# A two-layer graph network on Trainium2: the leaky step of layer 1 on ScalarE and GpSimd, the halves of q and k on GpSimd, three pieces of work in other slots

## The chip, the cores and the metric

The kernel runs on one core of one Trainium2 chip. The metric is the time of one execution in microseconds (us), the median of several runs; lower is better. A core has five engines, each with its own queue of instructions that it works through in order: TensorE (PE in the profile, its weight loads apart as PEld), VectorE (DVE), ScalarE (ACT), GpSimd (POOL) and SyncE (SP, which here only issues DMAs). An instruction waits, with everything behind it on its engine, until the semaphores that it names have been raised.

## The reference

The input is x (16 graphs, 1024 nodes, 256 features, fp32) and an adjacency matrix of zeros and ones (16 x 1024 x 1024, int32). Two layers run, each on a normed input with a residual:

```python
h = jnp.maximum(_layernorm(x), 0.0)           # layer 0: attention with 8 heads of 32
Q, K, V = proj(Wq, bq), proj(Wk, bk), proj(Wv, bv)
scores = where(adj == 0, -inf, einsum('bhnd,bhmd->bhnm', Q, K) * SCALE)
x = x + einsum('bno,po->bnp', softmax(scores) @ V, Wo) + bo
h = jnp.maximum(_layernorm(x), 0.0)           # layer 1: scores from a_0, leaky relu, slope 0.2
e = leaky_relu(einsum('bid,bjd->bij', h * a_0[:, 0], h), 0.2)
x = x + softmax(where(adj == 1, e, -9e15)) @ h
```

Kinds of edges above 1 (a_1 to a_3) would need further scores; a general path behind a test at the end (`layer_1_of_kinds`) covers them and does not run for these inputs.

## The kernel before

Layer 0's unit of work is an attention tile: 128 rows (queries) of one graph, all 8 heads, 1024 columns (`Attend`). There are 16 x 8 = 128 of them, and the main loop takes one *step* for each (`for s in range(B * NT + 1)`; t is the tile's number in its graph, 0 to 7). Within a step `for h in range(HEADS)` goes through the heads. For each head TensorE makes the scores of 128 x 1024 in one of two PSUM tiles called sides (`scores`, L455: two matmuls of 512 columns), DVE reads that side, scales, masks and finds the row maximum (`softmax_max`, L467), ScalarE exponentiates (`softmax_exp`, L475), and the result is transposed: for heads 2, 3, 6, 7 by TensorE with two copies of ScalarE (`turn`, L574 and L575), for heads 0, 1, 4, 5 by a DVE block transpose (`turn_blocks`, L376) and four DMAs of SyncE (`place_blocks`, L381). `combine` (L510) multiplies by the values, for heads 0 to 3 at h = 7 and for heads 4 to 7 at h = 3 of the next step. Then follow `output` (L525), `residual` (L531) and the norm's statistics on DVE.

Three more kinds of work share the step. *Pieces* (`Piece`) prepare 128 rows of a later graph: load, norm, transpose, then projections of k, q and v. The projections of k and q are written as two fp32r parts, a rounded high part by ScalarE (`high`, L289) and the rest by DVE (`split`, L294). They go to DRAM (k twice, once by SyncE at L321 and once by GpSimd in `write_again`; q by `write_queries`, L315) and come back in another layout (`load_key`, L356; `load_queries`, L422). *Layer 1's norm*: `norm_of`, 18 small GpSimd instructions on the statistics of one layer 0 tile and one piece together; then `normed` on ScalarE (L542), `turn_normed` on TensorE (L549), `turned_normed` on ScalarE (L553). *Edge tiles* (`Edges`) are layer 1's 128 rows, nine steps behind layer 0; in a step with tile t, the edge tile is number t - 1 of its graph (7 for t = 0). Its scores fill one side in two halves (`score`, L610 and L616: blocks left of the diagonal are transposed from copies kept in `mirror`, the rest are matmuls); `keep` (L630, ScalarE) copies blocks to `mirror`; `softmax_max` (L639, DVE) writes the negated scores y = -e, masked with a very large number, to `sel` and the smallest y of a row to `top`; `leak` (L647, DVE) makes min(0.2 y, y), that is, the negated leaky relu. Then come the exponential (L651), the block transpose and placements, `gather` (L669) and `store` (L678).

The order is written by hand (`tc.manual_schedule()`): each engine's queue holds its instructions in the order of the Python calls, nothing is moved later. Two sides for nine score tiles a step mean that the edge tile holds side 1 from after head 7 of the step before until its DVE pass and mirror copies are done, and heads 0, 1, 2 share side 0 meanwhile. Buffers set further waits: `blocks` has three, `sel`, `adj` and `xb` one each.

At t = 7 and t = 0, the *batch boundary*, GpSimd also issues the eight key loads of the next graph (512 KB each), at places set by `KEY_STEPS` (2h for the start and 2h + 1 for the end of head h; 16 and more lie in the t = 0 step). Before the loop lies a prologue; in the first nine steps there are no edge tiles; after the loop eight edge tiles are left, which run alone.

## Time and profile before

| | |
|---|---|
| time, median of 3 runs | 3197.36 us (3194.01 to 3206.88) |
| the profiled execution's own time | 3201.33 us |
| its span in the profile | 3199.5 us |
| PE busy | 2955.3 us (92%) |
| DVE busy | 2797.0 us (87%) |
| ACT busy | 2509.5 us (78%) |
| POOL busy | 1755.1 us (55%) |
| granted TensorE clock, mean | 0.987 |
| first and last residual addition (L531, one a step) | 101.0 and 3120.6 us |

The span is the time from the first instruction to the last in the profiled execution. Between the first and the last residual addition lie 127 steps, so a step takes 23.8 us on average. Cut at each step's first score matmul, the steps of batches 2 to 13 take, for t = 0 to 7: 24.87, 24.37, 24.33, 23.86, 23.34, 23.12, 23.34 and 25.44 us on average. A row of grouped instructions gives the line, the engine, the operation, the tiles written and read, the shape and the count, then the busy time and the mean of one in ns, then the idle time of the engine just before them and what ended it. In a timeline the first number is the start in us from the span's beginning, the second the duration. Ends of matmuls are modelled, so PE's busy time can cover a short wait.

### The profile page before, as it was taken

The page shows a single profiled execution, that of the slowest core. Times are in us where ns is not written, and L with a number is a line of the kernel's source. Part 1 is how long each engine was busy: PE and PEld are TensorE (multiplying, and loading weights), DVE is VectorE, ACT ScalarE, POOL GpSimd, SP SyncE. Part 2 cuts the span into 40 slices and gives each one's busy share as a digit, 9 for nine tenths or more (in the row PEclk, how much of TensorE's full clock was granted, in tenths as well). Part 3 has the DMA queues.
Part 4 walks back from the last instruction along what each step waited for, and adds up shares of the span by engine and source line. Part 5 has one row for each costly group of instructions (what it writes and reads, how often), then busy time and mean ns, then how long its engine had stood idle before and what let it go on. Part 6 is the DMA issues. An engine that isn't in the chain of part 4 may idle for free. (4 is left out here: it accounts for less than half of the span.)

```text
span 3199.5 us, 98068 instructions
## 1 busy us (share of the span) xinstructions
PE 2955.3 (92%) x36210; PEld 2215.4 (69%) x36210; DVE 2797.0 (87%) x5111; ACT 2509.5 (78%) x5037; POOL 1755.1 (55%) x3883
## 2 busy tenths in 40 slices
PE   5878999999999999989999999999999999998897
PEld 3666767777776777767767677777777767676664
DVE  3888989989898998989989899898989889898884
ACT  2888878888787888878888788888888788787772
POOL 2555555655555565555655555565565555555442
PEclk8999999999999999999999999999999999999999
DMA  6787787888878788787878888788787878878663
GB/s 225 223 248 228 233 263 225 265 237 233 268 234 274 223 250 254 228 262 234 264 236 237 273 229 279 223 246 261 230 279 227 252 235 240 266 226 269 175 189 94
DMA packets 747157, 762.93 MB, mean 238 GB/s; under 512 B 71280, under 2 KB 692208, under 8 KB 746672
## 3 DMA queue, kind: packets, MB, share of 16 engines
q1 hardware_dynamic: 678432, 542.34, 58.1%
q0 software_dynamic: 65040, 210.03, 20.7%
q8 instruction: 291, 4.77, 0.6%
q10 hardware_dynamic: 3200, 4.19, 0.4%
q14 instruction: 194, 1.59, 0.1%
HBM read 252.98 MB, written 167.77 MB: 132 GB/s over the span
## 5 line engine op out<-in xcount | busy, mean ns | idle before, releaser
L475 ACT ACTIVATE p<-p,nmx 128x1024 f32<-128x1024 f32 x1024 | 1183.4, 1156 | 246.5 <-DVE nmx L467 244.8
L467 DVE CUSTOM_DVE_ANT_0 p<-s,neg 128x1024 f32<-128x1024 f32 x1024 | 1232.9, 1204 | 94.7 <-issue 58.6
L455 PE MATMUL s<-k,qt 128*128 128x512 f32 x2048 | 786.1, 465 | 134.5 <-DMA qt<-qd 59.9
L435 POOL TENSOR_SCALAR neg<-adj 128x1024 bf16<-128x1024 int32 x128 | 467.1, 3649 | 378.7 <-ACT neg L447 378.5
L376 DVE STREAM_TRANSPOSE blocks<-p 128x1024 f32<-128x1024 f32 x520 | 642.9, 1236 | 12.2 <-ACT p L651 10.6
L575 ACT COPY pT<-trp 128x512 f32<-128x512 f32 x1024 | 546.5, 586 | 106.6 <-PE trp L574 103.9
L510 PE MATMUL acc<-pT,v 128*32 128x128 f32 x16384 | 527.2, 275 | 29.1 <-DMA pT<-blocks 27.9
L574 PE MATMUL trp<-ident,p 128*128 128x128 f32 x4096 | 536.0, 274 | 0.3 <-ACT pT L575 0.3
L574 PEld LDWEIGHTS trp<-ident,p 128*128 128x128 f32 x4096 | 483.1, 141 | 71.5 <-issue 1.8
L455 PEld LDWEIGHTS s<-k,qt 128*128 128x128 f32 x2048 | 327.6, 191 | 293.7 <-issue 96.5
L510 PEld LDWEIGHTS acc<-pT,v 128*32 128x32 f32 x16384 | 449.6, 110 | 103.5 <-issue 42.9
L669 PE MATMUL acc<-h,pT 128*32 128x256 f32 x8192 | 504.3, 383 | 15.4 <-DMA pT<-blocks 7.9
L669 PEld LDWEIGHTS acc<-h,pT 128*32 128x32 f32 x8192 | 244.4, 110 | 225.4 <-issue 59.4
L494 POOL COPY wide<-rec 128x256 f32<-128x256 f32 x128 | 51.1, 399 | 478.2 <-DVE rec L492 471.0
L321 POOL DMA_DIRECT2D kd<-halves x240 | 169.1, 704 | 257.6 <-DVE halves L294 244.6
L616 PE MATMUL s<-h1T,ha 128*128 128x512 f32 (+2 forms) x744 | 277.5, 496 | 8.6 <-ACT mirror L630 8.0
L639 DVE CUSTOM_DVE_ANT_0 sel<-s,neg 128x1024 f32<-128x1024 f32 x120 | 146.5, 1221 | 87.8 <-ACT p L475 59.7
L475 ACT ACTIVATION_READ_ACCUMULATOR p<-p,nmx 128x1 f32 x1024 | 199.1, 194 | 0.0
L616 PEld LDWEIGHTS s<-h1T,ha 128*128 128x128 f32 x744 | 122.9, 191 | 73.9 <-issue 46.2
L273 PEld LDWEIGHTS acc<-hT,wkT 128*128 128x128 f32 x960 | 118.4, 194 | 76.7 <-issue 46.5
L273 PE MATMUL acc<-hT,wkT 128*128 128x128 f32 x960 | 141.6, 291 | 27.4 <-DVE halves L294 26.2
L630 ACT COPY mirror<-s 128x128 f32<-128x128 f32 (+3 forms) x208 | 76.3, 395 | 103.0 <-DVE top L639 90.8
(129 smaller groups left out, 4237.7 us busy)
## 6 DMA issues: line engine op xcount, KB each, us to landing
pT<-blocks SPq DMA_DIRECT2D x2560, 128.0 KB, 3.1
qt<-qd SPq DMA_DIRECT2D x128, 512.0 KB, 5.9
adj<-in_adj POOLq DMA_DIRECT2D x127, 512.0 KB, 5.4
qd<-halves SPq DMA_DIRECT2D x240, 256.0 KB, 4.3
k<-kd POOLq DMA_DIRECT2D x120, 512.0 KB, 6.8
kd<-halves POOLq DMA_DIRECT2D x240, 128.0 KB, 3.5
kd<-halves SPq DMA_DIRECT2D x240, 128.0 KB, 3.2
xb<-in_x POOLq DMA_DIRECT2D x128, 128.0 KB, 3.4
```

The source lines that it names most:

```text
L273: nc.tensor.matmul(ps, lhsT=wT[:, fc, oc * P : (oc + 1) * P], rhs=(self.hT, self.hTm)[which][:, fc, :], start=(fc == 0), stop=(fc == NC - 1),)
L321: queue.dma_start(out=kds[self.b][oc, :, :, twice, self.cols], in_=halves.rearrange("p (w n) -> p w n", w=2),)
L376: nc.vector.transpose(blocks.rearrange("p b j q -> p j b q"), p)
L435: nc.gpsimd.tensor_scalar(self.neg, self.adj, 0.0, MASKED, ALU.is_equal, ALU.mult)
L455: nc.tensor.matmul(self.ps[:, cols], lhsT=self.qt[:, h, :], rhs=keysets[self.b][h][:, cols], start=True, stop=True,)
L467: nc.vector.tensor_tensor_reduce(out=p, in0=sides[h in (3, 5, 7)], in1=self.neg, scale=-SCALE, scalar=FLOOR, op0=ALU.add, op1=ALU.min, acc ...
L475: nc.scalar.activation(p, p, AF.Exp, bias=nmx, scale=-1.0, accum_out=self.sums[:, h : h + 1])
L510: nc.tensor.matmul(sums_place[r * HD : (r + 1) * HD, g * P : (g + 1) * P], lhsT=vs[self.b][:, j, place_of(h) : place_of(h) + HD], rhs=self ...
L574: nc.tensor.transpose(tr[:, j, :], p[:, jj * P : (jj + 1) * P], ident)
L575: copy(pT[:, half * 4 : half * 4 + 4, :], tr)
L616: nc.tensor.matmul(self.side[:, cols], lhsT=self.ha[:, c, :], rhs=h1T[:, c, cols], start=(c == 0), stop=(c == NC - 1),)
L669: nc.tensor.matmul(sums_place[a * HD : (a + 1) * HD, :], lhsT=self.pT[:, j, a], rhs=h1s[self.b][:, j, :], start=(j == 0), stop=(j == NT - 1),)
```

## The change

The change has five parts.

1. *The leaky step* of all edge tiles but the last eight. `softmax_max` now scales by -0.2, so `sel` holds z = 0.2 y (still the masked ones a very large number). The result wanted is min(z, 5 z) = z - relu(-4 z). `bend` makes relu(-4 z) with one ScalarE activation into a new tile `less` (a turn of the `blocks` buffers); `leak` subtracts it on GpSimd, after two tiny GpSimd instructions that do the same for the row's smallest value. The two DVE instructions (L644, L647) go. The last eight keep DVE's form.
2. *The halves of q and k.* In the loop, `high` and `split` give way to `raised` (ScalarE writes the biased projection, both chunks, to `full`) and `halve` (GpSimd copies `full` to the fp32r high part and subtracts). k's two chunks are now written by SyncE and GpSimd together at h = 0. Buffers of `halves`: 2 of double size instead of 4.
3. *Layer 1's scores*: the second half at h = 2 instead of 1, the DVE pass at h = 3 instead of 2, the mirror copies at h = 1 and 3 instead of 1 and 2; side 1 now goes to heads 4 and 6 (before: 3, 5, 7).
4. *q's projection* at h = 1 instead of 3, its ScalarE and GpSimd parts at h = 4.
5. *The norm of layer 1*: ScalarE's `normed` at h = 0 of the next step instead of h = 7, the transposes at h = 1 instead of 0 and in another PSUM quarter, the copy at h = 2 instead of 1.

```diff
--- before.py
+++ after.py
@@ -207,7 +207,7 @@
             tag = self.tags[i]
             if tag == "pT":
                 return ptp.tile(shape, dtype, tag=tag, name=tag)
-            bufs = {"p": 4, "blocks": 3, "halves": 4, "qt": 2, "xin": 2}.get(tag, 1)
+            bufs = {"p": 4, "blocks": 3, "halves": 2 if self.n == 1 else 4, "qt": 2, "xin": 2}.get(tag, 1)
             return work.tile(shape, dtype, tag=tag, name=tag, bufs=bufs)
         def load(self, queue=nc.gpsimd):
@@ -310,6 +310,25 @@
             else:
                 self.queries.append((oc, halves))
+        def raised(self, which):
+            self.full = work.tile([P, NC, P], F32, tag="full", name="full", bufs=1)
+            for _ in range(NC):
+                _, oc, ps, bias = self.projected.pop(0)
+                nc.scalar.activation(self.full[:, oc], ps, AF.Identity, bias=bias[:, oc : oc + 1])
+        def halve(self, which):
+            halves = self.buffer(3, [P, NC, 2, P], F32R)
+            nc.gpsimd.tensor_copy(halves[:, :, 0], self.full)
+            nc.gpsimd.tensor_tensor(halves[:, :, 1], self.full, halves[:, :, 0].bitcast(F32), ALU.subtract)
+            places = [(oc, halves[:, oc].bitcast(F32).rearrange("p w n -> p (w n)")) for oc in range(NC)]
+            if which == 0:
+                for oc, place in places:
+                    self.write_keys(oc, place, nc.sync, 0)
+                self.again = places
+            else:
+                self.queries = places
         def write_queries(self):
             for oc, halves in self.queries:
                 nc.sync.dma_start(
@@ -449,7 +468,7 @@
             )
         def scores(self, h):
-            self.ps = sides[h in (3, 5, 7)]
+            self.ps = sides[h in (4, 6)]
             for nh in range(N // HALF):
                 cols = slice(nh * HALF, (nh + 1) * HALF)
                 nc.tensor.matmul(
@@ -465,7 +484,7 @@
             p = work.tile([P, N], F32, tag="p", bufs=4)
             nmx = small.tile([P, 1], F32, tag="nmx")
             nc.vector.tensor_tensor_reduce(
-                out=p, in0=sides[h in (3, 5, 7)], in1=self.neg, scale=-SCALE, scalar=FLOOR,
+                out=p, in0=sides[h in (4, 6)], in1=self.neg, scale=-SCALE, scalar=FLOOR,
                 op0=ALU.add, op1=ALU.min, accum_out=nmx,
             )
             self.probs[h] = (p, nmx)
@@ -544,7 +563,7 @@
             )
         def turn_normed(self):
-            tr = by_chunk(early)
+            tr = by_chunk(brief)
             for c in range(NC):
                 nc.tensor.transpose(tr[:, c, :], h1s[self.b][:, self.t, c * P : (c + 1) * P], ident)
             self.h1_ps = tr
@@ -579,7 +598,7 @@
         def __init__(self, b, t, last=False):
-            self.b, self.t = b, t
+            self.b, self.t, self.last = b, t, last
             self.rows = slice(t * P, (t + 1) * P)
             self.side = sides[t % 2 if last else 1]
             self.tags = {"sel": ("p", 4), "pT1": ("pT", 7)} if last else {}
@@ -635,16 +654,28 @@
         def softmax_max(self):
             self.sel = self.buffer("sel", [P, N])
-            top = small.tile([P, 1], F32, tag="top")
+            self.top = small.tile([P, 1], F32, tag="top")
             nc.vector.tensor_tensor_reduce(
-                out=self.sel, in0=self.side, in1=masks[self.b, self.t], scale=-1.0, scalar=3e38,
-                op0=ALU.add, op1=ALU.min, accum_out=top,
-            )
+                out=self.sel, in0=self.side, in1=masks[self.b, self.t], scale=-SLOPE, scalar=3e38,
+                op0=ALU.add, op1=ALU.min, accum_out=self.top,
+            )
+        def bend(self):
+            if not self.last:
+                self.less = work.tile([P, N], F32, tag="blocks", name="less", bufs=3)
+                nc.scalar.activation(self.less, self.sel, AF.Relu, scale=1 - 1 / SLOPE)
+        def leak(self):
             self.nmx = small.tile([P, 1], F32, tag="nmx1")
-            nc.vector.scalar_tensor_tensor(self.nmx, top, SLOPE, top, ALU.mult, ALU.min)
-        def leak(self):
-            nc.vector.scalar_tensor_tensor(self.sel, self.sel, SLOPE, self.sel, ALU.mult, ALU.min)
+            if self.last:
+                for to, y in ((self.nmx, self.top), (self.sel, self.sel)):
+                    nc.vector.scalar_tensor_tensor(to, y, 1 / SLOPE, y, ALU.mult, ALU.min)
+            else:
+                less = small.tile([P, 1], F32, tag="less1")
+                nc.gpsimd.tensor_scalar(less, self.top, 0.0, 1 / SLOPE - 1, ALU.min, ALU.mult)
+                nc.gpsimd.tensor_tensor(self.nmx, self.top, less, ALU.add)
+                nc.gpsimd.tensor_tensor(self.sel, self.sel, self.less, ALU.subtract)
         def softmax_exp(self):
             self.total = small.tile([P, 1], F32, tag="total")
@@ -801,7 +832,7 @@
         piece_was.turned()
         for oc in range(NC):
             piece_was.project(0, oc)
-            piece_was.high()
+        piece_was.raised(0)
         gone = was = None
         for s in range(B * NT + 1):
@@ -824,10 +855,8 @@
                 if now:
                     now.scores(h)
                 if h == 0 and piece_was:
-                    piece_was.split()
-                if h == 1 and piece_was:
-                    piece_was.split()
-                if h == 2 and edge:
+                    piece_was.halve(0)
+                if h == 3 and edge:
                     edge.softmax_max()
                 if h == 5:
                     if was:
@@ -836,8 +865,6 @@
                 if h == 6 and edge_was:
                     edge_was.gather(1)
                 if h == 6 and piece_was:
-                    piece_was.split()
-                    piece_was.split()
                     piece_was.write_queries()
                 if now:
                     now.softmax_max(h)
@@ -845,23 +872,19 @@
                     edge_was.store()
-                if h == 4 and edge:
-                    edge.leak()
+                if h == 1 and edge:
+                    edge.keep(0)
+                if h == 2 and gone:
+                    gone.turned_normed()
                 if ending:
                     ending.softmax_exp(eh)
-                if h == 1 and gone:
-                    gone.turned_normed()
-                if h in (1, 2) and edge:
-                    edge.keep(h - 1)
+                if h == 3 and edge:
+                    edge.bend()
+                    edge.keep(1)
                 if h == 3:
-                    if piece_was:
-                        piece_was.project(1, 0)
-                        piece_was.project(1, 1)
                     if was:
                         was.combine(1)
                     if piece_was:
@@ -882,13 +905,16 @@
                     if edge:
                         edge.score(0)
                     if gone:
-                        gone.turn_normed()
+                        gone.normed()
                     if edge_was:
                         edge_was.turn_blocks()
                         edge_was.place_blocks()
                 if h == 1:
-                    if edge:
-                        edge.score(1)
+                    if gone:
+                        gone.turn_normed()
+                    if piece_was:
+                        piece_was.project(1, 0)
+                        piece_was.project(1, 1)
                     if was:
                         was.reciprocals()
                     if piece_nxt:
@@ -896,6 +922,8 @@
                     if piece_was:
                         piece_was.write_again()
                 if h == 2:
+                    if edge:
+                        edge.score(1)
                     if piece_was:
                         piece_was.values()
                     if was:
@@ -907,11 +935,17 @@
                 if h == 3:
                     if nxt:
                         nxt.load_queries()
+                    if edge:
+                        edge.leak()
+                    if nxt:
                         nxt.flag()
                         nxt.mask()
                 if h == 4:
                     if was:
                         was.output()
+                    if piece_was:
+                        piece_was.raised(1)
+                        piece_was.halve(1)
                     if piece:
                         piece.normed()
                     if edge_nxt:
@@ -923,9 +957,6 @@
                         edge_was.gather(0)
                     if piece:
                         piece.turn()
-                    if piece_was:
-                        piece_was.high()
-                        piece_was.high()
                     if piece:
                         piece.turned()
                 if h == 6:
@@ -942,10 +973,7 @@
                     if now:
                         now.combine(0)
                     if piece:
-                        piece.high()
-                        piece.high()
-                    if was:
-                        was.normed()
+                        piece.raised(0)
                 load_keys(h, 1)
             gone, was, now, nxt = was, now, nxt, nxt2
             edge_was, edge = edge, edge_nxt
@@ -953,6 +981,7 @@
+        gone.normed()
         gone.turn_normed()
         gone.turned_normed()
         tiles = [edge_was, edge] + [edges_of(B * NT + LAG - NT + t) for t in range(1, NT)]
@@ -972,6 +1001,7 @@
                 edge.keep(0)
                 edge.keep(1)
                 edge.softmax_max()
+                edge.bend()
                 edge.leak()
                 edge.softmax_exp()
             if i + 1 < len(tiles):
```

## The prediction

> **What bounds the kernel now.** I read the page's busy shares first: PE 92%, DVE 87%, ACT 78%, POOL 55%. The chain that ended last tells nothing here: the last stage alone ends it. So I cut the main loop into steps (one step is one attention tile; a step starts at its first score matmul) and asked for the busy time of each engine by step. One batch, t = 1 to 7, then t = 0 of the next:
>
> ```profile
> core 0: us, PE busy (x) PEld busy (x) DVE busy (x) ACT busy (x) POOL busy (x), PEclk, DMA share, GB/s
> 1421.30:1446.00 24.70, 24.21 (x289) 17.68 (x288) 21.68 (x40) 20.12 (x43) 13.49 (x29) 1.00 0.75 217
> ...
> 1494.10:1517.40 23.30, 22.81 (x288) 17.28 (x287) 22.18 (x42) 19.68 (x41) 13.02 (x29) 1.00 0.82 232
> ...
> 1563.50:1588.10 24.60, 21.21 (x281) 16.36 (x279) 21.49 (x41) 19.40 (x39) 16.51 (x35) 1.00 0.91 278
> 1588.10:1612.20 24.10, 22.76 (x289) 17.40 (x287) 21.53 (x41) 19.19 (x38) 14.27 (x31) 1.00 1.02 344
> ```
>
> DVE is busy 22.2 of 23.3 us at t = 4, but PE has 22.8 too: taking work from DVE can win only PE's waits. In the last two rows, where the next batch's keys are loaded, the DMA share reaches 1.02. PE's timeline over heads 1 to 3 of a t = 5 step shows where it waits (the brackets understate it: the modelled ends of L455's 1.02 and L500's 0.38 run into the waits):
>
> ```profile
> 1518.65 0.73 PE L455 MATMUL s<-k,qt 128*128 128x512 f32 x2 [0.46 <-DVE nmx L467]
> 1519.21 1.03 PE L574 MATMUL trp<-ident,p 128*128 128x128 f32 x8
> 1520.09 1.88 PE L616 MATMUL s<-h1T,ha 128*128 128x512 f32 x4
> 1521.40 1.02 PE L455 MATMUL s<-k,qt 128*128 128x512 f32 x2
> 1522.26 0.60 PE L340 MATMUL acc<-wvT,hTm 128*128 128x128 f32 x4
> 1522.70 0.61 PE L340 MATMUL acc<-wvT,hT 128*128 128x128 f32 x4
> 1523.15 0.38 PE L500 MATMUL acc<-ident,wide 128*128 128x128 f32 x2
> 1523.81 0.73 PE L455 MATMUL s<-k,qt 128*128 128x512 f32 x2 [0.27 <-ACT mirror L630]
> 1524.38 1.05 PE L273 MATMUL acc<-hTm,wqT 128*128 128x128 f32 x8
> ```
>
> From such lines I take what each piece of PE work costs from its start to the next start: a score pair 0.57, eight transposes 0.87, two 0.22, four edge matmuls of 512 columns 1.3 to 1.7, values 0.90, q's projection 0.95, a combine 1.88, the output 0.68, half a gather 1.86. From score to score, h = 3 to 7 take 3.43, 2.12, 3.68, 3.42 and 2.60 us in nearly every step, just these sums: PE never waits there. It waits in h = 0, 1 and 2: for the DVE pass that empties the side, and at h = 3 for ScalarE's mirror copy (L630), which frees the other side. The score-to-score times less the sums give 1.30, 1.55, 1.60, 1.24, 1.40 and 1.30 us of PE waits for t = 1 to 6: all there is to win outside the batch boundaries.
>
> **The change, part by part.**
>
> ```profile
> L647 DVE SCALAR_TENSOR_TENSOR sel<-sel 128x1024 f32<-128x1024 f32 x120 | 146.4, 1220 | 0.0
> ...
> L439 POOL TENSOR_TENSOR xb<-xb,bo_t 128x256 f32<-128x256 f32 x128 | 110.8, 866 | 0.0
> ...
> L644 DVE SCALAR_TENSOR_TENSOR nmx<-top 128x1 f32<-128x1 f32 x128 | 53.3, 417 | 4.5
> ...
> L494 POOL COPY wide<-rec 128x256 f32<-128x256 f32 x128 | 51.1, 399 | 478.2 <-DVE rec L492 471.0
> ```
>
> DVE, each step: less L647 (1.22), L644 (0.42) and four splits (L294, 0.31 and 0.35 each, 1.32): 2.96 us of 22.1 go. DVE is then done with time to spare and stops setting anything; the waits of h = 0 and 1 shrink to about 0.1.
>
> ScalarE: four activations of 128x128 stay four (L289, 0.37); new is one relu of 128x1024, by L475's row about 1.06 to the next start. 19.6 + 1.1 = 20.7 us, under PE's. But its place counts. The order on ScalarE becomes reciprocals' copy, head 2's exponential, relu, mirror copy, and the mirror copy frees the side that head 4's scores now need. From head 2's scores on PE: 0.57 + 1.72 + 0.90 + 0.43 to the end of the reciprocals' transposes = 3.62; copy 0.28, exponential 1.15, relu 1.06, mirror copy 0.59 and 0.05 of signalling: 6.75. PE has work for 0.57 + 1.72 + 0.90 + 0.22 + 0.57 + 1.88 = 5.86. New wait 0.88 us a step, in place of h = 3's old 0.85 to 1.05. At t = 6 (edge tile 5: shorter matmuls and a shorter mirror copy) it is 0.6. Late next: mask flag, head 3's exponential and the pT copies that free the transposes' PSUM, worth 0.1 at h = 5. Waits after: 1.0 for t = 1 to 5, 0.75 at t = 6. Gain: 0.30 + 0.55 + 0.60 + 0.24 + 0.40 + 0.55 = 2.64 us a batch.
>
> GpSimd: the subtraction of 128x1024 is shown nowhere. By L439, 0.87 for 256 elements beside 0.20 for two (L172) is 2.64 ns each: 2.9 us. L439's shortest, with DVE idle, is 0.72: 2.3. The upper bound is the mask's row (L435), 3.65. The Trainium skill (GPSIMD Engine Reference, Elementwise — side-by-side cycle accounting) states 4497 ns for 2048, so 2.3 to 2.5 as an estimate, and advises against such work on GpSimd as twice DVE's time; the row makes it 2.4 times. I take 2.9, since DVE is busy then; the page's value would change my sum by under 2 us, because the queue, not the length, matters. Also two tiny ones at 0.28, and twice copy (0.40, L494) plus subtraction (0.87): 2.9 + 0.6 + 2.5 = 6.0. With 13.0 busy now and 1.3 of gaps among the norm's 18 small instructions: 20.3 us of a 22.7 us step. It fits, with a ring through it: subtraction 2.9, mask 3.7, q's halves 1.3, edge queries 0.95, adjacency issue 0.6, norm 5.05, ScalarE's norm 0.6, PE's two transposes (h = 1), and 7.3 more over q's projection, head 2's scores, reciprocals, exponential and relu back to the subtraction: 22.4 us. PE's steps after the gain are 24.1 to 22.6: the ring is just hidden. At 3.65 it is 23.2 and paces t = 4 to 6.
>
> A rule that speaks against: the same skill (SBUF — State Buffer, Who interferes with whom) has GpSimd and a DVE instruction of two SBUF inputs exclude each other for a whole instruction. The trace agrees: L644 takes 0.16 in the median and up to 1.19 beside L439. By the rule a 2.9 us subtraction would hold DVE that long. By the rows nothing is left in the loop to hold: L647 and L644 leave, all passes over scores read PSUM, and L376 keeps 1.24 beside L439. I take 0; against me, DVE's 3 us of slack cover one such hold.
>
> SyncE: k's two writes now wait for GpSimd's halves (about 4 to 5 us into the step, against 1.3 and 7), and behind them are the four placements of the edge tile; these are needed at h = 5, 15 us in. The relu's tile takes a turn in the three blocks buffers, so head 1's DVE transpose waits for that placement to land, about 11 to 12 us in, when it is due at 11.3. Cover: DVE's slack. The other moves (norm, transposes of the norm, edge scores, q's projection) issue as many instructions as before, in slots with work around them: 0.
>
> **Batch boundary.** GpSimd issues eight key loads there, and each stands behind its queue:
>
> ```profile
> 1597.22 3.65 POOL L435 TENSOR_SCALAR neg<-adj 128x1024 bf16<-128x1024 int32 x1 [0.96 <-ACT neg L447]
> 1600.94 0.61 POOL L356 DMA_DIRECT2D k<-kd  x1
> ...
> DMA to landing us min/median/max: 5.5/6.9/8.3
> ```
>
> The last load follows the mask, 13.6 us after the step's first scores (1587.3); it lands at 19.7, and head 7's scores run at 20.5: almost no slack. With 6 us more in front of it, it is issued at about 17.5 and lands at 23.5. The loads at the end of t = 7 come 5 to 6 us later as well. Against that, queries landing late cost 3.2 us at the end of t = 7 now, beside four key loads; with the loads later those queries land sooner. t = 7 and 0 together are 50.3 us now; I get t = 7 shorter by 2 to 3 and t = 0 longer by 2 to 3. I take +0.4, ends -1.5 and +5.5.
>
> **Sum.** 15 batches x -2.64 = -39.6; 14 boundaries x 0.4 = +5.6: -34 us. First nine steps and the tail of eight edge tiles: 0 (the tail keeps DVE's leak). The profiled execution took 3201.3 (span 3199.5): 3167. The median of the runs is 4.0 lower: 3163.
>
> **Rivals.**
> Forecast: a small gain, 3163. Chance 0.41.
> PE's floor: the mirror copy comes early enough and all waits of h = 0 to 4 fall to 0.2: -7.2 a batch, 3090. For it: h = 3 to 7 already run without waits. Against: the order on ScalarE puts relu before the copy. 0.07.
> Wash: the subtraction is nearer 3.65, the ring paces t = 4 to 6 (gain 1.85 a batch) and boundaries lose 2.7: +10, 3207. The change then does what it says and DVE's relief ends in GpSimd's queue. 0.21.
> Slower: the last key load alone. If it is issued 20 us into t = 0, it lands at 26 to 27 and head 7 waits 6: 14 x 6 = 84 less 39.6, about 3242. It decides from 2.8 us lost per boundary on. For it: the slack now is under 1 us, and DMA is full there. Against: the queries' stall overlaps with it. 0.31.
>
> **How the numbers follow.** The likeliest is 3163; gains alone span 3090 to 3180. A tenth on either side leaves 3110 to 3245. 0.5% (16 us, about what a measurement of this kernel can tell) puts the bounds at 3181 and 3213: faster 0.46 (forecast and floor, less a little), same 0.22, slower 0.32.
>
> **What would show it.** Right: DVE busy near 19.2 a step; PE's wait at head 4 for the mirror copy of 0.6 to 0.9, h = 0 and 1 nearly without; subtraction near 2.9; GpSimd at 20 us. Wrong: ScalarE's norm waiting on GpSimd in most steps (the ring paces), scores waiting on key loads by over 3 us, DVE instructions stretched beside the subtraction, or placements landing so late that gather waits.

## The result, and the profile after

The changed kernel takes 3234.85 us (median of 4 runs, 3228.61 to 3239.68) against 3195.69 us of the kernel before beside it (3191.6 to 3206.88): the ratio is 1.0116, with a 95% interval of 1.0081 to 1.015. It is 1.2% slower. The prediction was 3163 us, a gain of 1.1%.

The head of the page shows that the change did what it says. Compared with before, DVE's busy time falls by 280 us and GpSimd's rises by 588 us:

```profile
span 3237.8 us, 97791 instructions
PE 2972.1 (92%) x36210; PEld 2211.2 (68%) x36210; DVE 2516.9 (78%) x4391; ACT 2576.2 (80%) x5157; POOL 2342.7 (72%) x4723
```

The loss is found by cutting the main loop into steps again, at each step's first score matmul. Mean length in us, steps 9 to 118:

| | t=0 | 1 | 2 | 3 | 4 | 5 | 6 | 7 |
|---|---|---|---|---|---|---|---|---|
| before | 24.89 | 24.39 | 24.31 | 23.87 | 23.37 | 23.08 | 23.26 | 25.62 |
| after | 30.34 | 24.46 | 23.59 | 23.27 | 23.00 | 23.13 | 22.79 | 24.57 |

Summed over the loop, the steps t = 1 to 6 (from step 9 on) went from 2125.6 to 2094.3 us, 31 us less. The steps t = 7 and 0 (15 pairs, from step 7 on) went from 752.1 to 817.1 us, 65 us more. The last step and the tail took 5 us more. Together these make up the 38 us between the two spans, to within 1 us. So the steps between the boundaries became shorter, much as predicted, and the boundaries took back twice that.

The busy time by step, for a t = 1, a t = 4, a t = 7 and the t = 0 after it:

```profile
core 0: us, PE busy (x) PEld busy (x) DVE busy (x) ACT busy (x) POOL busy (x), PEclk, DMA share, GB/s
1434.90:1459.20 24.30, 23.77 (x284) 16.92 (x282) 19.49 (x35) 20.47 (x44) 17.45 (x33) 1.00 0.84 253
1506.10:1529.10 23.00, 22.60 (x290) 17.05 (x286) 19.57 (x35) 20.04 (x41) 18.09 (x37) 1.00 0.81 236
...
1769.80:1794.10 24.30, 22.00 (x288) 17.25 (x285) 19.61 (x35) 20.30 (x41) 20.25 (x43) 1.00 0.81 239
1794.10:1824.90 30.80, 23.43 (x286) 18.34 (x286) 19.12 (x35) 19.71 (x40) 21.29 (x44) 0.89 0.85 291
```

No engine but PE is near the length of a step. In the last row not even PE is: 23.4 of 30.8 us. That step loses its time to waits. PE's timeline over heads 0 to 4 of a t = 5 step shows the other side, a step that works well:

```profile
1529.10 0.73 PE L474 MATMUL s<-k,qt 128*128 128x512 f32 x2
...
1531.25 0.73 PE L474 MATMUL s<-k,qt 128*128 128x512 f32 x2
...
1533.72 0.70 PE L474 MATMUL s<-k,qt 128*128 128x512 f32 x2
...
1537.00 0.71 PE L474 MATMUL s<-k,qt 128*128 128x512 f32 x2
1537.71 2.16 PE L529 MATMUL acc<-pT,v 128*32 128x128 f32 x64
1540.16 0.73 PE L474 MATMUL s<-k,qt 128*128 128x512 f32 x2 [0.29 <-ACT mirror L649]
```

The waits of heads 0 and 1 are gone. The only one left is at head 4, for the mirror copy, where the prediction put it. On ScalarE the mirror copy stands behind relu, and the mask's flag (L466) and the copies of the turned probabilities (L594) come after it:

```profile
1538.70 1.05 ACT L667 ACTIVATE less<-sel 128x1024 f32<-128x1024 f32 x1
1539.64 0.47 ACT L649 COPY mirror<-s 128x384 f32<-128x384 f32 x1
1540.00 1.16 ACT L466 ACTIVATE neg<-adj,less_half 128x1024 bf16<-128x1024 int32 x1
...
1541.15 1.14 ACT L494 ACTIVATE p<-p,nmx 128x1024 f32<-128x1024 f32 x1
...
1542.28 1.06 ACT L594 COPY pT<-trp 128x512 f32<-128x512 f32 x2
```

The costs in the groups of instructions:

```profile
L678 POOL TENSOR_TENSOR sel<-sel,less 128x1024 f32<-128x1024 f32 x120 | 285.7, 2381 | 142.5 <-ACT less L667 142.5
...
L323 POOL TENSOR_TENSOR halves<-full,halves 128x256 fp32r<-128x256 f32 x240 | 176.4, 735 | 20.6
...
L395 DVE STREAM_TRANSPOSE blocks<-p 128x1024 f32<-128x1024 f32 x520 | 644.8, 1240 | 152.7 <-DMA pT<-blocks 140.4 <-ACT p L682 10.7 <-ACT recT L523 1.3
```

The third row is the telling one. Before, it read:

```profile
L376 DVE STREAM_TRANSPOSE blocks<-p 128x1024 f32<-128x1024 f32 x520 | 642.9, 1236 | 12.2 <-ACT p L651 10.6 <-DMA pT<-blocks 1.2
```

DVE stood 12.2 us in front of its block transposes, 1.2 of them for a placement DMA. Now it stands 140.4 us there, waiting for DMAs that still read a `blocks` buffer. About half of it (67 us) falls in the 30 boundary steps, the rest in the 90 others. What that does to a boundary can be followed in the timeline of all engines over the t = 0 step that is the last row of the table of busy times:

```profile
1797.29 4.33 SPq L400 DMA_DIRECT2D pT<-blocks  x4
...
1797.63 0.70 PE L474 MATMUL s<-k,qt 128*128 128x512 f32 x2 [1.50 <-DMA k<-kd]
...
1803.14 1.18 DVE L658 CUSTOM_DVE_ANT_0 sel<-s,neg 128x1024 f32<-128x1024 f32 x1
...
1803.46 0.70 PE L474 MATMUL s<-k,qt 128*128 128x512 f32 x2 [0.79 <-DMA k<-kd]
...
1809.52 1.06 ACT L667 ACTIVATE less<-sel 128x1024 f32<-128x1024 f32 x1 [5.30 <-DMA pT<-blocks]
1809.55 3.63 PE L529 MATMUL acc<-pT,v 128*32 128x128 f32 x62 [5.05 <-DMA pT<-blocks]
1810.65 2.37 POOL L678 TENSOR_TENSOR sel<-sel,less 128x1024 f32<-128x1024 f32 x1 [5.70 <-ACT less L667]
1813.10 3.66 POOL L454 TENSOR_SCALAR neg<-adj 128x1024 bf16<-128x1024 int32 x1
1816.83 0.61 POOL L375 DMA_DIRECT2D k<-kd  x1
```

DVE has written `sel` by 1804.3. Relu could start, but its tile needs a `blocks` buffer, and the placements that read the oldest one have not landed: ScalarE stands for 5.3 us. Behind relu in ScalarE's queue is the mirror copy; behind relu through a semaphore is GpSimd's subtraction, and behind that in GpSimd's queue are the mask and the last key load, which goes out 22.7 us into the step. PE stands beside them for placements of its own (5.05 us).

This step is one of the worst. In 8 of the 14 steps t = 0 with a relu, relu stands for a placement; over all 14 it waits 2.0 us on average, and 5.3 is the longest wait. The last key load of a boundary goes out 20.4 us into the t = 0 step in the median (17.2 to 23.0), against 13.6 before.

PE's idle time by cause over the 26 boundary steps among steps 9 to 118 says how much each is: 67.3 us before (30.2 for queries, 29.3 for placements, 5.7 for DVE's passes, 2.0 for keys) and 105.5 us after (38.3 for placements, 33.8 for keys, 14.7 for queries, 14.2 for the residual `x`, which is late because DVE was). These sums understate the waits, since modelled ends of matmuls run into them.

### The profile page after: what moved, and what is told of

Its sections match the earlier page's. It is cut to its first block, busy times and chain, and to the rows that moved or that the text cites. A ratio compares the mean times of both kernels' runs of the same rounds, so it can differ in the third digit from the quotient of the medians.

```text
span 3237.8 us, 97791 instructions
## 1 busy us (share of the span) xinstructions
PE 2972.1 (92%) x36210; PEld 2211.2 (68%) x36210; DVE 2516.9 (78%) x4391; ACT 2576.2 (80%) x5157; POOL 2342.7 (72%) x4723
## 5 line engine op out<-in xcount | busy, mean ns | idle before, releaser
L474 PE MATMUL s<-k,qt 128*128 128x512 f32 x2048 | 766.8, 456 | 145.0 <-DMA qt<-qd 53.5
L395 DVE STREAM_TRANSPOSE blocks<-p 128x1024 f32<-128x1024 f32 x520 | 644.8, 1240 | 152.7 <-DMA pT<-blocks 140.4
L594 ACT COPY pT<-trp 128x512 f32<-128x512 f32 x1024 | 548.4, 590 | 134.1 <-PE trp L593 133.7
L529 PE MATMUL acc<-pT,v 128*32 128x128 f32 x16384 | 552.7, 280 | 42.8 <-DMA pT<-blocks 41.1
L529 PEld LDWEIGHTS acc<-pT,v 128*32 128x32 f32 x16384 | 469.3, 112 | 157.8 <-issue 89.6
L593 PE MATMUL trp<-ident,p 128*128 128x128 f32 x4096 | 549.8, 278 | 2.3 <-ACT pT L594 2.1
L678 POOL TENSOR_TENSOR sel<-sel,less 128x1024 f32<-128x1024 f32 x120 | 285.7, 2381 | 142.5 <-ACT less L667 142.5
L523 ACT COPY recT<-acc 128x256 f32<-128x256 f32 x128 | 47.7, 373 | 205.3 <-PE acc L519 205.3
L323 POOL TENSOR_TENSOR halves<-full,halves 128x256 fp32r<-128x256 f32 x240 | 176.4, 735 | 20.6
L635 PEld LDWEIGHTS s<-h1T,ha 128*128 128x128 f32 x744 | 127.7, 192 | 72.0 <-issue 45.6
L676 POOL TENSOR_SCALAR less<-top 128x1 f32<-128x1 f32 x120 | 29.8, 248 | 176.7 <-DVE top L658 175.4
```

The costliest lines, as they stand in the source:

```text
L323: nc.gpsimd.tensor_tensor(halves[:, :, 1], self.full, halves[:, :, 0].bitcast(F32), ALU.subtract)
L395: nc.vector.transpose(blocks.rearrange("p b j q -> p j b q"), p)
L474: nc.tensor.matmul(self.ps[:, cols], lhsT=self.qt[:, h, :], rhs=keysets[self.b][h][:, cols], start=True, stop=True,)
L529: nc.tensor.matmul(sums_place[r * HD : (r + 1) * HD, g * P : (g + 1) * P], lhsT=vs[self.b][:, j, place_of(h) : place_of(h) + HD], rhs=self ...
L593: nc.tensor.transpose(tr[:, j, :], p[:, jj * P : (jj + 1) * P], ident)
L594: copy(pT[:, half * 4 : half * 4 + 4, :], tr)
```

## The experiments

Two theories stood at the start. *Key loads* (the slower rival, widened): the subtraction and its queue push key loads back, and that is the boundary's 65 us. *Blocks turn*: relu's tile in `blocks` makes ScalarE and DVE wait for outgoing DMAs. A third question was what the parts are worth alone.

All runs in one table; the boundary column is t = 7 and 0 from step 7, the other t = 1 to 6 from step 9, both of the profiled execution (turn_only's took 3206 us, 15 under its median, so its two columns are low). The kernel before took 3204 us beside these runs, 3208 beside room_only and 3196 beside the changed kernel itself.

| run | us | ratio to before, 95% | t = 1 to 6 | boundaries |
|---|---|---|---|---|
| before | 3204 | 1 | 2125.6 | 752.1 |
| after | 3235 | 1.0116 (1.0081 to 1.015) | 2094.3 | 817.1 |
| keys_early | 3213 | 1.0030 (1.002 to 1.0041) | 2096.3 | 791.7 |
| before_keys_late | 3307 | 1.0319 (1.0294 to 1.0344) | 2117.6 | 861.2 |
| mirror_first | 3237 | 1.0117 (1.0076 to 1.0158) | 2094.3 | 814.0 |
| mirror_keys | 3216 | 1.0026 (1.0005 to 1.0047) | 2100.8 | 790.5 |
| own_less | 3181 | 0.9936 (0.9912 to 0.9959) | 2085.9 | 764.9 |
| room_only | 3271 | 1.0175 (1.0129 to 1.0221) | 2106.7 | 833.0 |
| leak_on_dve | 3127 | 0.9767 (0.9731 to 0.9803) | 2042.2 | 757.1 |
| turn_only | 3221 | 1.0059 (1.0037 to 1.0081) | 2077.1 | 805.3 |
| halves_dve | 3202 | 0.9991 (0.9978 to 1.0003) | 2100.7 | 771.9 |
| flag_early | 3186 | 0.9939 (0.9924 to 0.9955) | 2081.1 | 783.1 |
| best | 3124 | 0.9759 (0.9729 to 0.9789) | 2040.6 | 755.9 |
| best_dve | 3132 | 0.9768 (0.9752 to 0.9784) | 2041.5 | 765.0 |

### The key loads: keys_early and before_keys_late

keys_early is the changed kernel with the loads issued at earlier heads:

```diff
-    KEY_STEPS = (6, 9, 10, 13, 16, 20, 22, 24)
+    KEY_STEPS = (6, 6, 6, 8, 10, 16, 20, 22)
```

> The changed kernel with the eight key loads of the next graph earlier in GpSimd's queue: loads 0 to 2 at head 3 of the t = 7 step, 3 at head 4, 4 at head 5, 5 at head 0 of the t = 0 step, 6 and 7 at heads 2 and 3. Nothing else moves. Theory A (the boundary's loss comes from key loads that leave GpSimd's longer queue 5 to 7 us later and meet the pT placements): t = 7 and t = 0 together fall from 55 us to about 50, 14 boundaries give 55 to 65 us, 3170 to 3185 us. Rival B (the placements are late because SyncE waits for GpSimd's halves, or because the relu's tile takes a blocks buffer): boundaries stay at 54 to 55, 3225 us or more. Rival C (the last load alone, as the prediction had it): the wait before head 7 goes and 10 to 20 us with it, 3215 to 3225; the waits before heads 1 to 4 stay.

It took 3213 us, between the ranges of theory A and rival C. PE's waits for keys at the boundaries fell from 33.8 us to none, and the boundaries lost 25 of the 65 us; waits for placements (46.6) and for the residual (19.0) stayed and grew a little. Late key loads are a real part, and less than half.

before_keys_late asks the reverse: the kernel before, its loads put as late as the changed kernel issues them or somewhat later.

```diff
-    KEY_STEPS = (6, 9, 10, 13, 16, 20, 22, 24)
+    KEY_STEPS = (7, 12, 13, 17, 18, 21, 22, 28)
```

> The kernel before with nothing changed but the places of the eight key loads in GpSimd's queue, put later so that they are issued about when the changed kernel issues them (first after the mask of head 3, then 3 us before the t = 0 step, at 2, 8 and 21 us in it). Theory A: the boundaries grow from 50 to about 54 or 55 us, 3240 to 3260 us. Rival B: without the GpSimd halves and without the relu's tile nothing is lost, 3190 to 3210 us.

3307 us, far more than the change itself costs. The chain of waits of this run has

```profile
PE s L455 <- DMA k<-kd: 101.1, 35, 8.3
```

(total us, times, longest) where the changed kernel has

```profile
PE s L474 <- DMA k<-kd: 39.9, 23, 3.9
```

So a late key load is as dear as the slower rival said: in 12 steps t = 0, head 7 waits 4 to 8 us for it. But the changed kernel has less than half of this wait, and this run overshot its lateness (the last load goes out at 24.3 us in the median, not 20.4); it prices the mechanism and does not show that it is the cause.

### The mirror copy: mirror_first and mirror_keys

mirror_first lets the mirror copy go ahead of relu on ScalarE:

```diff
                 if h == 3 and edge:
-                    edge.bend()
                     edge.keep(1)
+                    edge.bend()
```

> The changed kernel with the mirror copy of head 3 ahead of the relu on ScalarE instead of behind it. If PE's wait at head 4 is the relu's place, the score-to-score time of head 3 falls from 3.27 to about 2.5 us in the steps t = 1 to 4 and less at 5 and 6; steps lose 0.3 to 0.8 us, 45 to 65 us in all, 3170 to 3190 us. If the ring through GpSimd paces these steps, another wait (ScalarE's norm for GpSimd, or PE for that norm) takes its place and less than 10 us come: 3225 us or more.

3237 us, no change. At t = 4 the stretch from head 3's scores to head 4's fell from 3.27 to 2.79 us, so the wait did go. The stretch from head 5's to head 6's grew from 3.76 to 4.24: PE now waits for ScalarE's copies of the turned probabilities (18.9 us in all) behind relu and the mask's flag. The same 0.48 us moved along ScalarE's queue. What costs is how much stands in that stretch of the queue, relu among it, and not the order of relu and mirror copy.

mirror_keys has both edits.

> Both edits: mirror copy ahead of the relu, and the key loads early. If the two losses are apart, the gains add: 3105 to 3130 us, below the kernel before. If GpSimd's queue is the bound behind both, one gain swallows the other: 3165 us or more.

3216 us, the same as keys_early alone.

### The blocks turn: own_less, room_only, leak_on_dve, turn_only

own_less gives relu's tile a buffer of its own (bf16 for want of space, which makes layer 1's result less exact; two small tiles share other buffers to make room):

```diff
-                self.less = work.tile([P, N], F32, tag="blocks", name="less", bufs=3)
+                self.less = work.tile([P, N], BF16, tag="less", name="less", bufs=1)
...
-            self.wide = work.tile([P, HEADS, HD], F32, tag="wide", bufs=1)
+            self.wide = work.tile([P, HEADS, HD], F32, tag="h0", name="wide", bufs=1)
...
-            self.oT = work.tile([P, NC, P], F32, tag="oT", bufs=1)
+            self.oT = work.tile([P, NC, P], F32, tag="hT", name="oT", bufs=1)
```

> The changed kernel with the relu's tile in a buffer of its own (in bf16, since no room is left for fp32, so the result of layer 1 is less exact; two small tiles share other tiles' buffers to make room), instead of a turn of the three blocks buffers. If that turn is part of the boundary's loss (DVE's block transpose of head 1 waits for the edge tile's placement, the residual and with it PE come late), PE's 14 us of waiting for the residual and the 140 us of DVE waiting for placements go, 15 to 25 us in all: 3210 to 3222 us. If the key loads and the full DMA alone make the loss: 3228 us or more.

3181 us, 54 less than the changed kernel, 29 better than the range expected, and 0.6% faster than before. DVE's group row becomes

```profile
L395 DVE STREAM_TRANSPOSE blocks<-p 128x1024 f32<-128x1024 f32 x520 | 643.9, 1238 | 11.3 <-ACT p L682 10.7
```

The 140 us of waits are gone, and the boundaries are back at 764.9 us. PE's waits for keys stay at 36.8 us in the boundary steps; those for the residual and the queries are gone there, and those for placements fall from 38.3 to 26.2. ScalarE still waits for DVE's `sel` before relu, but stands there only 0.2 us on average at t = 0 instead of 2.0, so that dependence alone is not what costs. One thing besides the turn changed with it: the bf16 operand made the subtraction shorter, 2147 ns. The two edits that make room are the other suspects; room_only makes them alone.

> The control for own_less: the changed kernel with only the two edits of place that made room there (wide takes h0's buffer, oT takes hT's), relu's tile staying in blocks. Theory A, the blocks turn made own_less faster and these edits did nothing: within 10 us of the changed kernel, 3225 to 3245, boundary steps about 817. Theory B, the edits took part in it: below 3215, and the turn's price at the changed kernel is smaller than the 54 us that own_less showed by as much.

3271 us: these edits alone cost 36 us by the medians and some 19 by the ratios (0.0059 of 3204). Neither theory had that. So own_less gained in spite of them, and measured against room_only the turn, with the shorter subtraction, is worth 77 us (ratios 1.0175 and 0.9936) rather than 54. Why sharing those two buffers costs so much was not followed up; DVE's waits for placements rose with it:

```profile
L395 DVE STREAM_TRANSPOSE blocks<-p 128x1024 f32<-128x1024 f32 x520 | 644.9, 1240 | 189.4 <-DMA pT<-blocks 177.5 <-ACT p L682 10.7 <-DMA kd<-halves 0.3
```

leak_on_dve takes relu and the subtraction away altogether: the leaky step is DVE's two instructions again (at the changed kernel's place), everything else stays changed.

```diff
         def bend(self):
-            if not self.last:
+            if False:
...
         def leak(self):
-            if self.last:
+            if True:
```

> The changed kernel with the leaky step of all edge tiles back on DVE (two DVE instructions, no relu, no GpSimd subtraction); halves on GpSimd and all new slots stay. ScalarE loses 1.06 us and GpSimd 2.9 us a step, DVE gains 1.4. If relu and subtraction are what is too much: PE's wait at head 4 falls from 0.8 to about 0.3 us (about 45 us over the loop) and the boundaries lose 2 us less each (about 30 us): 3160 to 3190 us, below the kernel before. If the halves on GpSimd or the new slots make the loss: 3225 us or more.

3127 us, 2.3% faster than before and 33 us better than the range expected. The steps t = 1 to 6 fall to 2042.2 us, with only 11.0 us of PE's waits left in the steps between boundaries up to step 118 (before 62.9, after 49.1). The part of the change that was to take the most from DVE is the part that loses.

turn_only is leak_on_dve plus the turn, and nothing else of relu: ScalarE writes one column of a `blocks` tile that nobody reads.

```diff
-            if False:
+            if not self.last:
                 self.less = work.tile([P, N], F32, tag="blocks", name="less", bufs=3)
-                nc.scalar.activation(self.less, self.sel, AF.Relu, scale=1 - 1 / SLOPE)
+                nc.scalar.activation(self.less[:, :1], self.sel[:, :1], AF.Relu, scale=1 - 1 / SLOPE)
```

> leak_on_dve (3127 us) with the turn of the blocks buffers put back and nothing else: where relu stood, ScalarE writes one column of a blocks tile that nobody reads; the leaky step stays on VectorE, and nothing waits for the column. Theory A, the turn itself is what costs: ScalarE stands at its turn behind the edge's placement at each boundary, VectorE's next transpose gets its buffer one placement later, and the boundary steps go from 757 us back to 795 or more; time 3160 to 3185. Theory B, the turn costs only through the subtraction, the mask and the key load that queue behind relu on GpSimd (here nothing of GpSimd queues behind it): boundaries stay within 15 us of 757, time below 3145.

3221 us, 94 more than leak_on_dve, for an instruction of 0.19 us. Theory A's direction and place hold, its size was too low. The DVE row in leak_on_dve:

```profile
L395 DVE STREAM_TRANSPOSE blocks<-p 128x1024 f32<-128x1024 f32 x520 | 643.8, 1238 | 13.4 <-ACT p L682 10.7 <-DMA pT<-blocks 2.0
```

and in turn_only, with one row of PE that says where the delay came out:

```profile
L395 DVE STREAM_TRANSPOSE blocks<-p 128x1024 f32<-128x1024 f32 x520 | 644.6, 1240 | 139.5 <-DMA pT<-blocks 127.7 <-ACT p L682 10.6 <-DMA kd<-halves 0.4
...
L243 PE MATMUL acc<-ident,h 128*128 128x128 f32 x240 | 51.9, 298 | 56.1 <-DVE x L550 55.3 <-ACT h L229 0.4
```

DVE waits 127.7 us for buffers instead of 2.0; the passes and the residual addition behind it are late, the piece's transposes on PE wait for that residual, and PE stands 55.3 us there (0.8 in leak_on_dve; 15.9 in the changed kernel, where more of the delay comes out at placements and keys). The four corners: without the turn 3127 (leak on DVE) and 3181 (relu and subtraction, own_less), with it 3221 and 3235. The turn costs 94 where nothing else is slow, 54 to 77 where relu and the subtraction are in place. Relu and the subtraction cost up to 54 without it (the room edits included) and 14 on top of it: their delays overlap.

### The halves: halves_dve

leak_on_dve with the halves of q and k on DVE, so that only the new places of the work remain.

```diff
-            nc.gpsimd.tensor_copy(halves[:, :, 0], self.full)
-            nc.gpsimd.tensor_tensor(halves[:, :, 1], self.full, halves[:, :, 0].bitcast(F32), ALU.subtract)
+            nc.vector.tensor_copy(halves[:, :, 0], self.full)
+            nc.vector.tensor_tensor(halves[:, :, 1], self.full, halves[:, :, 0].bitcast(F32), ALU.subtract)
```

> leak_on_dve (3127 us) with the copy and the subtraction that make the halves of q and k on VectorE instead of GpSimd. All that is then left of the change are the places of the work: layer 1's scores one head later, q's projection and the norm in other steps, k's halves together. Theory A, the relief of VectorE is what gained: VectorE gets back some 1.5 us in each step and the time goes to 3155 to 3190. Theory B, the places gained and GpSimd does little for it: below 3140.

3202 us: the same time as the kernel before, and 12 us above the range of theory A. The places alone bring nothing (25 us less in the steps, 20 more at the boundaries). The halves on GpSimd then bring 72 us (ratios 0.9991 and 0.9767). The heads of the two pages, halves_dve:

```profile
PE 2958.6 (92%) x36210; PEld 2207.9 (69%) x36210; DVE 2809.0 (88%) x5111; ACT 2491.2 (78%) x5037; POOL 1749.9 (55%) x3883
```

and leak_on_dve:

```profile
PE 2942.1 (94%) x36210; PEld 2212.7 (71%) x36210; DVE 2635.5 (84%) x4631; ACT 2479.7 (79%) x5037; POOL 2001.1 (64%) x4363
```

1.4 us less of DVE in each step (174 us in all) took PE's waits for DVE's passes between the boundaries from 42.8 to 3.5 us, and more that the modelled ends hide. After that, DVE is no longer what PE waits for, and the further 1.0 us of DVE a step that the leaky step frees (2635.5 to 2516.9 us busy) has nothing left to win.

### Mending the change: flag_early, best, best_dve

flag_early puts GpSimd's mask and the adjacency load ahead of the subtraction, with ScalarE's flag a head earlier (it also has the two edits of room and one more mask buffer):

```diff
                 if h == 2:
...
                     if piece_was:
                         piece_was.values()
+                    if nxt:
+                        nxt.flag()
...
                     if edge_was:
                         edge_was.load_nodes()
+                    if nxt:
+                        nxt.mask()
+                    if nxt2:
+                        nxt2.load()
```

> The changed kernel with the mask's flag on ScalarE ahead of the reciprocals' copy at head 2 (where ScalarE idles 1.6 us), the mask on GpSimd ahead of the leaky step, and the next adjacency load right behind it, some 5 us earlier (one more mask buffer, two small tiles share buffers to make room). If GpSimd's lateness at its DMA issues is the boundary's cause, PE's boundary waits fall by 15 to 35 us: 3200 to 3220 us, and the wait at head 4 stays. If it is not: 3230 us or more.

3186 us, better than expected: against the changed kernel the boundaries lose 34 us and the steps 13. It does so in spite of the two edits of room; against room_only, which has them too, it is 76 us by the ratios (1.0175 and 0.9939), less what the further mask buffer may add. best has this, the early key loads, the mirror copy ahead of relu, and SyncE's key writes issued behind the edge tile's placements instead of ahead of them:

```diff
+        def write_once(self):
+            for oc, place in self.once:
+                self.write_keys(oc, place, nc.sync, 0)
...
                     if edge_was:
                         edge_was.turn_blocks()
                         edge_was.place_blocks()
+                    if piece_was:
+                        piece_was.write_once()
```

> flag_early with the mirror copy ahead of the relu, the key loads early, and SyncE's two k writes behind the edge tile's placements. ScalarE's work between head 2's exponential and the pT copies of head 3 is then 1.13 us shorter, so that the wait does not move from head 4 to head 5 as it did when the mirror copy alone was moved: 0.5 us a step, about 50 us; with the boundaries 30 to 50 us better: 3130 to 3165 us, below the kernel before. If another engine's queue paces the steps: 3200 us or more.

3124 us, 6 better than the range expected, with a ratio of 0.9759: 2.4% faster than before, level with leak_on_dve and 3.5% faster than the changed kernel. The subtraction is no shorter, but nothing waits long in front of it: 1.3 us in all, against 142.5 in the changed kernel:

```profile
L680 POOL TENSOR_TENSOR sel<-sel,less 128x1024 f32<-128x1024 f32 x120 | 285.7, 2381 | 1.3 <-ACT less L669 1.3
...
L397 DVE STREAM_TRANSPOSE blocks<-p 128x1024 f32<-128x1024 f32 x520 | 644.3, 1239 | 70.5 <-DMA pT<-blocks 54.2 <-ACT p L684 10.7 <-ACT p L496 3.9
```

The turn is still there, but DVE's waits at it are down from 140.4 to 54.2 us. Between the boundaries the wait that mirror_first only moved is gone: in the t = 4 step the flag (1.16 us) now runs at head 2, where ScalarE waited for PE, and head 5's stretch is back at 3.68 us. How best's whole gain divides among its edits was not tested.

best_dve puts the leaky step of best back on DVE.

> best (3124 us) with the leaky step on VectorE again, so neither relu nor its blocks tile nor the subtraction; early key loads, the early flag and mask, the mirror copy first and the key writes behind the placements stay. Theory A, what the two versions mended is separate: the boundary steps fall from 756 us to 720 to 740 as the placements come earlier, the steps between stay at about 2040, time 3085 to 3110. Theory B, both had reached the same floor, set by the placements of the attention at a boundary, 60 us of TensorE's waits in best: 3115 to 3130.

3132 us, 2 us above the range of theory B; the intervals of the two ratios overlap. Theory B holds: both have 7 to 10 us of PE's waits left between the boundaries and 60 us of waits for placements in the boundary steps. At this floor it makes no difference which engine does the leaky step.

## Why the prediction was wrong

**The step that failed is the cover for the turn of `blocks`.** The prediction saw that relu's tile takes a turn, that head 1's transpose then waits for the edge tile's placement, and that this lands at 11 to 12 us when the transpose is due at 11.3. It wrote "Cover: DVE's slack" and priced it at nothing. Two things were wrong with that. DVE's queue is in order, so what stands behind the transpose is late as well, whatever DVE's mean load: the residual, whose lateness PE paid with 55.3 us in turn_only. And the 11 to 12 us were those of a step between boundaries. There the changed kernel's transpose waits little, on average 0.0 us at t = 1 and 1.5 at t = 6; at t = 7 it waits 2.9 and at t = 0 2.0 us. A placement takes 2.95 us in the median between the boundaries before the change and 5.2 us in boundary steps (a tenth take over 7.4). And at t = 0 ScalarE stands at the turn too, with relu, the mirror copy, the subtraction, the mask and a key load behind. The turn costs 54 to 94 us, depending on what else is in place. Without it, and with all else of the change (own_less), the time is 0.6% under before: the direction that was forecast, and about half of the size.

**The boundary's +0.4 us a time** was the second face of this error: it was 4.3 us a time (65.0 over 15). The prediction's upper end of 5.5 held it. The sum that it made, later key loads against queries that land sooner, was right in kind: PE's waits for queries at the boundaries fell from 30.2 to 14.7 us and those for keys rose from 2.0 to 33.8. The last load was later than the 17.5 us predicted: 20.4 us in the median. Left out were DVE's late residual and ScalarE's stall.

**The gain of 2.64 us a batch between the boundaries** was nearly right: 31.3 us in all against 39.6. The new wait at head 4 is there, with head 3's stretch at 3.27 us in the median for a sum of work of about 2.45 to 2.8, so 0.5 to 0.8 us against 0.88 predicted. But the gain was booked to the relief of DVE as a whole. halves_dve and leak_on_dve show that the halves alone had brought 58 us there, and that the leaky step then took 52 back (2042.2 to 2094.3), of which own_less puts 44 on relu and the subtraction themselves and room edits, and 8 on the turn; turn_only puts 35 on the turn alone, so the delays overlap here as well. The prediction had said itself that PE's waits are all there is to win; it did not ask which part of DVE's relief was enough to win them.

**Durations.** The subtraction took 2381 ns. The prediction took 2.9 us from L439's mean and had 2.3 from its shortest; the Trainium skill (GPSIMD Engine Reference, Elementwise — side-by-side cycle accounting) gave 2.3 to 2.5 as an estimate from its 4497 ns for 2048 elements, and this is where the measurement is. The halves took 405 ns for the copy and 735 for the subtraction, against 399 and 866. GpSimd is busy 17.5 to 18.1 us in the steps shown for t = 1 and 4, against 20.3 predicted with the gaps, and the ring did not pace them: ScalarE's norm waited for GpSimd 12 times, 17.2 us in all. The lock between GpSimd and DVE was priced at 0, and no cost of it shows: the transposes take 1240 ns (1236 before) and the edge tile's pass 1186 (1221). The stretches of the prediction's first table begin 0.8 to 1.5 us behind the steps' first score matmuls (1588.10 where the step starts at 1587.31); none of its sums rests on that.

**The rivals.** The slower rival had the place, the size (3242), the last load's time (20 us) and part of the mechanism. Its "last key load alone" is refuted: with no wait for keys left, keys_early is still at 3213. The wash by a ring through GpSimd did not occur. PE's floor of 3090 was not reached, but its assumption was: in best PE's waits between the boundaries are down to 6.6 us. That "relu before the copy" stands against it was half the truth, as mirror_first shows: relu's 1.05 us costs PE the same at two places of ScalarE's queue. With the mirror copy moved alone (mirror_first) the wait goes to another place; with the flag moved alone (flag_early) PE still waits 28 us for the mirror copy; with both (best) neither wait is left.

What stays open: how the 65 us divide exactly, since the causes overlap (25 us go with the key loads, 52 with the turn, 34 with the mask's place), how best's gain divides among its edits, and why sharing two small buffers costs 19 us or more.

## What to carry to other kernels

A tile that borrows a turn in a ring of buffers whose readers are DMAs ties the borrowing engine, and every engine that takes the next turns, to the landing of those DMAs; price it at the landing time of the busiest stage and list what stands behind each of the waiting engines. Before adding up what an offload takes from a busy engine, find how much of it removes the waits of the engine that sets the pace: the first 1.4 us a step here were worth 72 us, the next 1.0 nothing. And put on a helper's queue what others wait for (a mask, a load) ahead of long work that waits itself: with the flag, the mirror copy and the key writes moved as well, such places decided between 3235 and 3124 us.

## What the runs showed of the hardware

The granted clock of TensorE over the boundary steps was 0.979 before and 0.950 after, and 0.998 in the other steps of both. The lower clock goes with PE's waits. In steps 9 to 126 of the changed kernel there are 11 gaps of 3 us or more between PE's matmuls; with each, a stretch of 3.4 or 6.8 us at half the clock begins, during the gap or within 4 us of its end. Of the 15 gaps of 1.5 to 3 us this holds for nine. Before, it is 5 of 5 and 6 of 16. It does not explain the loss: leak_on_dve has 0.948 there and its boundary steps take 757 us.

The same DMA of 128 KB lands in 2.95 us in the median in steps whose mean DMA share is 0.78 and in 5.2 us where it is 0.94 (kernel before). GpSimd's fp32 subtraction of 1024 elements is 2381 ns with two fp32 operands and 2147 ns with one of them bf16.
